# Three sums of a block in one PSUM bank, and one copy of them in the next block

## The chip, the cores and the metric

One Trainium2 chip; the kernel runs on one of its cores. The metric is the time of one execution on the device, in microseconds. Engines are named as in the profile: PE multiplies matrices, PEld is its weight load, DVE is the vector engine, ACT the scalar engine, POOL issues the gathers, SP the other transfers.

## The reference

A graph layer on 6250 nodes with 64 features and 206250 edges, sorted by their destination:

```python
h = jnp.maximum(_layernorm(x, axis=-1), 0.0)
msg = h[src] + edge_attr
agg = jax.ops.segment_sum(msg, dst, num_segments=6250)
out = x + jax.nn.relu(agg @ W1 + b1) @ W2 + b2
```

All of it is fp32. The gather `h[src]` and the sum by destination are what costs.

## The kernel before, in words

The aggregate is kept turned round in SBUF (`agg`, two halves of 64 partitions by node) and is made of two terms. The features gathered from `h` are not gathered at all for most edges: the kernel counts on PE how often each source occurs among a triple of destinations, and multiplies these counts by `h`. The edge features are summed on PE with 0/1 matrices. The last 20 tiles of edges ("groups") go another way: POOL gathers their rows of `h` and adds them to the edge features in flight, and both are summed at once.

Nodes are handled in 23 blocks (`NW`), each of 14 steps (`STEPS`; the last block has 10). The order of all work is written out by hand, step by step, in the loop at the end of the kernel (`for n, (b, s) in enumerate(steps)`), and every engine takes its instructions in this order. In one step stand, in this order:

- `count(b, s)`: six matmuls into one of two PSUM buffers `pc` (L868), and one copy on ACT of 882 columns to the ring of counts (L871). Once in three steps, two comparisons on DVE make the 0/1 matrices for it (L858).
- `multiply(b - 1, ...)`: in steps 0 to 6, the 49 matmuls of the counts of the block before with `h` (L888), into the PSUM tile `pv`.
- `chunk_place` at step 3: twelve matmuls (L461) that put the sums of the edge features of the block before into `pv`, by a selection matrix. After it, at step 10, DVE adds `pv` to `agg`.
- the dense layers of a block that is complete: `mlp_hidden` at step 8 (and 11 if there are two), PE L936 and ACT L938; `mlp_product` two steps later, PE L943 and ACT L949.
- `chunk_sum` at steps 7, 10 and 13 (`SUMS`): the sums of edge features, below.
- `features_h`, at steps 0, 1, 2 or 4 (`GROUPS`) of some blocks, when the gathers have come in: the sum of two groups (PE L489, ACT L492), placed one to four steps later (PE L508, ACT `sum_p` L512).

`chunk_sum(u)` handles a unit of two chunks of 42 nodes: 24 matmuls (48 in the profile) of a 0/1 matrix (`hot`, by DVE, a step earlier) with edge features (`feat`, by SP, two units ahead) into the PSUM tile `bank`, and directly after them ACT copies 128 columns of it to an SBUF tile `by_node` (L442). A block has three units, so three sums and three such copies; the last block has two. `bank` is one tile of 128 columns, used by all units and by the groups in turn:

```python
bank = ps.tile([P, GB * D], F32, name="bank", bufs=1)
...
        by_node[u] = work.tile([P, GB, D], F32, name="by_node", bufs=3)
        nc.scalar.activation(by_node[u][:, :n].rearrange("p c d -> p (c d)"), bank[:, :n * D], AF.Copy)
        load(u + 2)
```

Other work on ACT has places by step number too: clearing `agg` (L162, in blocks 1 and 2), the copies that unpack and turn the keys (`klof` L704, `keys` L726), and checks (`junk` L694). The waits between the engines are put in by a layer that records which instruction touches which tile; for PSUM it keeps two engines apart by the bank.

Of the kernel before, what the change touches and what calls it, by code (L numbers as in the profile page):

```python
# [9 lines left out]
F32 = mybir.dt.float32  # L10
# [4 lines left out]
AF = mybir.ActivationFunctionType  # L15
# [4 lines left out]
P = 128  # L20
N = 6250
E = 206250
D = 64
# [14 lines left out]
GB = 2  # L38
# [8 lines left out]
WQ = 21  # L47
QP = 32
# [28 lines left out]
NW = 23  # L77
# [37 lines left out]
OPEN = 30  # L115
KR = 540
AHEAD = 16
OPENING_US = 15.0


@with_exitstack
def gnn_kernel(ctx: ExitStack, tc: tile.TileContext, x, src_t, dst_t, dst_g, edge, w1, b1, w2, b2, out):
    nc = tc.nc
# [8 lines left out]
    ps = ctx.enter_context(tc.tile_pool(name="ps", bufs=2, space=PSUM))  # L132
    work = ctx.enter_context(tc.tile_pool(name="work", bufs=2))
# [263 lines left out]

    bank = ps.tile([P, GB * D], F32, name="bank", bufs=1)  # L400
    nc.vector.memset(bank, 0.0)
    units = []
    for b in range(NW):
        c0, c1 = (start[b] // CN, min(start[b + 1], NS) // CN)
        units += [(b, c, min(c1 - c, GB)) for c in range(c0, c1, GB)]
    assert sum(n for _, _, n in units) == NC
    unplaced = [sum(1 for unit in units if unit[0] == b) for b in range(NW)]

    def load(u):
        if u >= len(units):  # L410
            return
        _, c, n = units[u]
        at = nc.values_load_multi_w_load_instructions(
            starts_i[0:1, c:c + n], engines=[mybir.EngineType.SP], min_val=0, max_val=G * P * J - CE,
            skip_runtime_bounds_check_because="sums of edges before, at most that by a min")[1]
        feats[u] = [work.tile([P, CT, D], F32, name="feat", bufs=4) for _ in range(n)]
        for k in range(n):
            nc.sync.dma_start(feats[u][k].rearrange("p (q k) d -> p q (k d)", q=JQ),
                              edge[ds(at[k], CE), :].rearrange("(q p k) d -> p q (k d)", p=P, k=JP))

    hot_of = {}
    by_node = {}
# [9 lines left out]
    def chunk_sum(u):  # L432
        n = units[u][2]
        hot, feat = hot_of.pop(u), feats.pop(u)
        for i in range(n):
            for k in range(JP):
                for q in range(JQ):
                    j = q * JP + k
                    nc.tensor.matmul(bank[q * QP:q * QP + WQ, i * D:(i + 1) * D], hot[:, i, j, :], feat[i][:, j, :],  # L439
                                     start=(k == 0), stop=(k == JP - 1))  # L440
        by_node[u] = work.tile([P, GB, D], F32, name="by_node", bufs=3)
        nc.scalar.activation(by_node[u][:, :n].rearrange("p c d -> p (c d)"), bank[:, :n * D], AF.Copy)  # L442
        load(u + 2)

    def column(b, node):
        i, half = node - start[b], NH if b < NW - 1 else HL
        return (i + half) % (2 * half) if 2 * b % 3 == 2 else i

    def runs(b, low, high):
        half = start[b] + (NH if b < NW - 1 else HL)  # L450
        cuts = sorted({low, high} | ({half} if low < half < high and 2 * b % 3 == 2 else set()))
        return [(column(b, a), a, z) for a, z in zip(cuts, cuts[1:])]

    def chunk_place(u):
        b, c, n = units[u]
        of = by_node.pop(u)
        unplaced[b] -= 1
        for i in range(n):
            low = (c + i) * CN
            for k, a, z in runs(b, low, low + CN):  # L460
                nc.tensor.matmul(pvs[b][0][i * D:(i + 1) * D, k:k + z - a], of[:, i, :], select[:, a - low:z - low],  # L461
                                 start=False, stop=False)
# [21 lines left out]
    def sum_groups(g, hot, tiles):  # L484
        for b in range(GB):
            for k in range(PK):
                for q in range(PQ):
                    j = q * PK + k
                    nc.tensor.matmul(bank[q * QP:q * QP + WQ, b * D:(b + 1) * D], hot[:, b, j, :],  # L489
                                     tiles[b][:, j, :], start=(k == 0), stop=(k == PK - 1))  # L490
        by_node["h", g] = work.tile([P, GB, D], F32, name="by_group", bufs=1)
        nc.scalar.activation(by_node["h", g].rearrange("p b d -> p (b d)"), bank, AF.Copy)  # L492

    sels = {}

# [38 lines left out]
    def fetch_pair(i0):  # L534
        n = min(2, IC - i0)
        fetch_words(i0, n, P, [first_i[:, i:i + 1] for i in range(i0, i0 + n)])
# [454 lines left out]
    def pool_until(us):  # L991
        while queue and pool[0] <= us:
            cost, f = queue.pop(0)
            pool[0] += cost
            f()

    def features_h(g):
        read_bases(g, GB)
        sum_groups(g, hot_groups(g), [parts_of.pop(g + b) for b in range(GB)])
        for b in range(GB):  # L1000
            fetch_h(g + 2 * GB + b)
# [70 lines left out]
    for k in range(1, (IC + 1) // 2):  # L1072
        n = (17, 58, 100, 142, 184, 226, 268)[k - 1]
        if k > 2:
            before.setdefault(n - AHEAD, []).append(
                lambda k=k: queue.insert(0, (WORDS_US, lambda: fetch_pair(2 * k))))
# [3 lines left out]
    for t in range(1, NT):  # L1080
        n = (0, 18, 101, 156, 226)[t]
# [8 lines left out]
    def clock(n):  # L1090

        return n * HEAD_US if n < STEPS else STEPS * HEAD_US + (n - STEPS) * STEP_US

    steps = [(b, s) for b in range(NW) for s in range(STEPS if b < NW - 1 else STEPS_L)]
    first_step = [steps.index((b, 0)) for b in range(NW)]
# [4 lines left out]
    SUMS, PLACES, LAYERS = (7, 10, 13), 3, (8, 11)  # L1100
    PRODUCTS = (5, 12, 19, 26, 33, 41, HI)
    PRODUCTS_L = (8, 18, 28, 39, HI)
    ADDED, LOADED = 10, 2
    LAST, LATE, SUMS_L = (3, 8), 7, (6, 8)
    ADDS = (6, 7)
    GROUPS, PLACED = (0, 1, 2, 4), (1, 2, 4, 5)
# [4 lines left out]
    def at(step, f, *a):  # L1111
        later.setdefault(step, []).append(lambda: f(*a))
# [8 lines left out]
    for u, (b, c, _) in enumerate(units):  # L1121
        i = u - min(v for v in range(u + 1) if units[v][0] == b)
        n = (10, 12, 13)[i] if b == 0 else first_step[b] + (SUMS if b < NW - 1 else SUMS_L)[i]
        places.setdefault(b, []).append(u)
        at(n - 1, chunk_hot, u)
        at(n, chunk_sum, u)

    h_next = GA

# [12 lines left out]
    for n, (b, s) in enumerate(steps):  # L1142
# [6 lines left out]
        if b >= 1 and s == (PLACES if b < NW - 1 else 2):  # L1149
            for u in places[b - 1]:  # L1150
                chunk_place(u)
# [4 lines left out]
        k = n - (first_step[SB + 1] + ADDED + 1)  # L1156
# [16 lines left out]
        if n >= 3:  # L1173
# [7 lines left out]
            if n == 3:  # L1181
                pool[0] = clock(n - 1) + OPENING_US
            pool_until(clock(n) + LAND_US)
# [31 lines left out]
    for u in places[NW - 1]:  # L1215
        chunk_place(u)
# [4 lines left out]
    if late_hot is not None:  # L1221
        sum_groups(h_next, late_hot, [parts_of.pop(h_next + b) for b in range(GB)])
# [16 lines left out]
    with tc.If(odd > 0):  # L1239
# [26 lines left out]
        with tc.For_i(0, G, 1) as g:  # L1266
            feat = work.tile([P, J, D], F32, tag="pfeat", bufs=4, name="feat2")
# [17 lines left out]
            with tc.For_i(0, more, 1) as w:  # L1285
                hot = work.tile([P, J, WR], F32, tag="pfeat", bufs=4, name="hotr")
# [7 lines left out]
                at = nc.s_assert_within(first_n + w * WR, 0, N + W - 1)  # L1294
# [44 lines left out]
```

## Time and profile before

| | |
|---|---|
| median of 3 runs | 489.25 us (488.44 to 490.86) |
| the profiled execution | 489.07 us, its span 487.2 us |
| PE busy | 424.2 us (87% of the span) |
| DVE busy | 415.1 us (85%) |
| POOL busy | 388.3 us (80%) |
| ACT busy | 366.0 us (75%) |
| copies of the sums, L442 | 68, together 19.0 us of ACT |

Busy time counts an instruction from its start to its end; on ACT and PE the next one overlaps the end of the one before, so the slots are shorter than the durations. Matmul ends are modelled. A wait is the idle time of an engine before an instruction, put down to what ended it. In the chain that ended last, each piece is what the next one had to wait for, back from the end of the execution. The first some 55 us are loads, the normalization and the sorting of the lists; the steps fill the rest.

### The profile page before, as it was taken

The numbers are of one execution on the slowest core, as the hardware profiler recorded it, in microseconds if no ns is written. First come the engines' busy times: TensorE is split into PE (matmuls) and PEld (weight loads), VectorE is DVE, ScalarE is ACT, GpSimd is POOL, SyncE is SP. The second block draws the span as 40 slices with busy tenths as digits, with TensorE's granted clock in tenths as the row PEclk, the third lists the DMA queues.
The fourth block names the chain that finished last, engine by engine and source line by source line (L and its number), as shares of the span: only waits on it lengthen the run. The fifth ranks groups of instructions, "written<-read, shape, count | busy, mean of one in ns | idle before, by whom it ended". The sixth has DMA issues, their size and how long they took to land.

```text
span 487.2 us, 17218 instructions
## 1 busy us (share of the span) xinstructions
PE 424.2 (87%) x7301; PEld 374.8 (77%) x7302; DVE 415.1 (85%) x561; ACT 366.0 (75%) x607; POOL 388.3 (80%) x239
## 2 busy tenths in 40 slices
PE   3156798998988999999999999989999999999894
PEld 3055687886886888888988978878888888888783
DVE  7888989879999798988998889888998899998751
ACT  3727889878877788788898789777887787786650
POOL 7787888888888888888888888888888888888000
PEclk9655699999999999999999999999999999999998
DMA  9959367378366585784784784675775775764700
GB/s 237 238 172 300 74 147 193 76 180 192 69 167 155 145 228 122 176 230 105 192 220 98 172 228 94 170 201 125 187 187 124 201 179 122 203 158 93 213 13 16
DMA packets 122378, 77.98 MB, mean 160 GB/s; under 512 B 34768, under 2 KB 120728, under 8 KB 122072
## 3 DMA queue, kind: packets, MB, share of 16 engines
q1 hardware_dynamic: 97464, 66.88, 47.1%
q0 software_dynamic: 24592, 9.19, 15.0%
q8 instruction: 59, 0.97, 0.8%
q10 hardware_dynamic: 240, 0.75, 0.5%
q14 instruction: 23, 0.19, 0.1%
HBM read 72.80 MB, written 3.99 MB: 158 GB/s over the span
## 4 chain that ended last, share of the span: by engine, by line
PE 68%; ACT 13%; DMA 6%; issue 5%; DVE 4%; POOL 3%; DVEq 0%; ACTq 0%; POOLq 0%
PE pv L888 26%; PE pc L868 22%; PE bank L439 11%; ACT counts L871 9%; POOL rows L301 3%; DMA feat<-in_edge 3%; PE po L943 2%; PE pv L461 2%; DMA dstq<-in_dst_g,cols_i 2%; ACT junk L694 1%; PE ph L936 1%; PE bank L489 1%; DVE hot_key L858 1%; DVE hot_lo L858 1%; DMA firsts_i<-in_dst_g 1%
## 5 line engine op out<-in xcount | busy, mean ns | idle before, releaser
L301 POOL DMA_INDIRECT pfeat<-table,src_p x160 | 334.0, 2088 | 49.7 <-issue 43.0
L871 ACT ACTIVATE counts<-pc 128x882 fp32r<-128x882 f32 x318 | 282.1, 916 | 49.1 <-PE pc L868 39.8
L868 PE MATMUL pc<-hot_key,hot_lo 128*128 128x147 bf16 x1908 | 179.2, 232 | 22.9 <-ACT counts L871 13.6
L858 DVE TENSOR_TENSOR hot_lo<-iota_lo,keys 128x2304 bf16<-128x2304 bf16 (+1 forms) x107 | 143.8, 1344 | 36.2 <-PE pc L868 29.0
L888 PE MATMUL pv<-counts,h 128*128 128x252 f32 (+1 forms) x1127 | 171.0, 292 | 0.2
L868 PEld LDWEIGHTS <-hot_lo 128*128 128x128 bf16 x1908 | 130.5, 100 | 45.4 <-issue 24.2
L858 DVE TENSOR_TENSOR hot_key<-iota_key,keys 128x2664 bf16<-128x2664 bf16 (+1 forms) x107 | 163.3, 1526 | 0.0
L888 PEld LDWEIGHTS pv<-counts,h 128*128 128x128 f32 x1127 | 143.5, 190 | 0.6 <-ACT counts L871 0.5
L439 PE MATMUL bank<-feat,hot 128*21 128x64 f32 x3240 | 69.0, 222 | 5.9 <-issue 3.0
L439 PEld LDWEIGHTS bank<-feat,hot 128*21 128x21 f32 x3240 | 52.3, 101 | 18.3 <-issue 6.8
L427 DVE TENSOR_TENSOR hot<-rel,iota 128x504 f32<-128x504 bf16 x68 | 45.6, 671 | 0.1
L442 ACT ACTIVATE by_node<-bank 128x128 f32<-128x128 f32 x68 | 19.0, 280 | 18.4 <-PE bank L439 12.4
L301 POOL DMA_INDIRECT words<-packed,first_i x15 | 20.8, 1385 | 4.6 <-issue 3.4
L301 POOL DMA_INDIRECT rows<-in_dst_g,row_i x15 | 17.4, 1162 | 5.2 <-issue 4.0
L943 PE MATMUL po<-w2s,hid 128*126 128x64 f32 (+2 forms) x100 | 16.8, 288 | 1.7 <-ACT hid L938 1.2
L943 PEld LDWEIGHTS po<-w2s,hid 128*126 128x126 f32 (+2 forms) x100 | 13.5, 192 | 5.7 <-ACT hid L938 1.9
L936 PE MATMUL ph<-sums,w1s 128*128 128x252 f32 (+2 forms) x50 | 16.1, 404 | 0.2 <-ACT y L949 0.2
L900 DVE TENSOR_TENSOR sums<-sums,pv 128x252 f32<-128x252 f32 (+4 forms) x31 | 9.8, 339 | 6.7 <-PE pv L888 5.9
L492 ACT ACTIVATE by_group<-bank 128x128 f32<-128x128 f32 x10 | 2.8, 277 | 15.1 <-PE bank L489 11.1
L938 ACT ACTIVATE hid<-ph,b1s 128x252 f32<-128x252 f32 (+2 forms) x25 | 11.6, 464 | 2.3 <-PE ph L936 2.3
L461 PE MATMUL pv<-select,by_node 128*64 128x42 f32 (+1 forms) x272 | 12.6, 234 | 0.0
L461 PEld LDWEIGHTS pv<-select,by_node 128*64 128x64 f32 x272 | 9.9, 137 | 3.0
(202 smaller groups left out, 252.3 us busy)
## 6 DMA issues: line engine op xcount, KB each, us to landing
feat<-in_edge SPq DMA_DIRECT2D x135, 384.0 KB
pfeat<-in_edge SPq DMA_DIRECT2D x20, 256.0 KB
pfeat<-table,src_p POOLq DMA_INDIRECT x160
xl<-in_x SPq DMA_DIRECT2D x2, 768.0 KB
xs<-in_x SPq DMA_DIRECT2D x23, 63.0 KB
out_y<-y SPq DMA_DIRECT2D x23, 63.0 KB
dstn<-in_dst_g SPq DMA_DIRECT2D x1, 1024.0 KB
table<-xl SPq DMA_DIRECT2D x1, 800.0 KB
```

The source lines that it names most:

```text
L301: nc.gpsimd.indirect_dma_start(out=rows, out_offset=None, in_=source, in_offset=bass.IndirectOffsetOnAxis(ap=index, axis=0), compute_op=op)
L427: nc.vector.tensor_tensor(hot_of[u][:, :n].rearrange("p c j w -> p (c j) w"), rel[:, c:c + n].rearrange("p c q k -> p (c q k)").unsqueeze( ...
L439: nc.tensor.matmul(bank[q * QP:q * QP + WQ, i * D:(i + 1) * D], hot[:, i, j, :], feat[i][:, j, :], start=(k == 0), stop=(k == JP - 1))
L442: nc.scalar.activation(by_node[u][:, :n].rearrange("p c d -> p (c d)"), bank[:, :n * D], AF.Copy)
L461: nc.tensor.matmul(pvs[b][0][i * D:(i + 1) * D, k:k + z - a], of[:, i, :], select[:, a - low:z - low], start=False, stop=False)
L858: nc.vector.tensor_tensor(hot[:, :n].rearrange("p t (m o) -> p t m o", o=2), iota_k.rearrange("p (m o) -> p m o", o=2).unsqueeze(1).to_bro ...
L868: nc.tensor.matmul(pc[:, k, m * K:(m + 1) * K], hot_lo[:, j, :], hot_key[:, j, :K], start=True, stop=True)
L871: nc.scalar.activation(ring[:, (2 * b + half) % 3, :, i * ST * V:(i + 1) * ST * V].rearrange("p h (k m) -> p h k m", k=2), pc[:, :, :ST // ...
L888: nc.tensor.matmul(pv[:, :2 * half].rearrange("p (k n) -> p k n", k=2), h2[:, h, :], of[:, :, h, :half], start=(h == 0), stop=(h == HI - 1))
L936: nc.tensor.matmul(ph[:, :n], w1s, agg[:, start[b]:start[b + 1]], start=True, stop=True)
L938: nc.scalar.activation(outs[b][:, :n], ph[:, :n], AF.Relu, bias=b1s)
L943: nc.tensor.matmul(po[:pairs[b], k, :], outs[b][:, k:2 * pairs[b]:2], w2s, start=True, stop=True)
```

## The change

`bank` becomes a full PSUM bank of four sets of 128 columns: three for the units of a block (`set_of[u]` is 0, 1 or 2), one for the groups. `chunk_sum` no longer copies. A new `chunk_copy` copies the sets of a block with one instruction of 384 columns into one tile `by_node[b]`. It stands at step 1 (`COPIED`) of the next block, behind that step's counts and ahead of a group's sum, two steps before `chunk_place` reads it. In the last block each unit is copied at its own step, as before. Loads and matmuls keep their steps.

```diff
-    bank = ps.tile([P, GB * D], F32, name="bank", bufs=1)
+    bank = ps.tile([P, SETS + 1, GB, D], F32, name="bank", bufs=1)
...
+    set_of = [sum(1 for v in units[:u] if v[0] == units[u][0]) for u in range(len(units))]
...
-                    nc.tensor.matmul(bank[q * QP:q * QP + WQ, i * D:(i + 1) * D], hot[:, i, j, :], feat[i][:, j, :],
+                    nc.tensor.matmul(bank[q * QP:q * QP + WQ, set_of[u], i, :], hot[:, i, j, :], feat[i][:, j, :],
                                      start=(k == 0), stop=(k == JP - 1))
-        by_node[u] = work.tile([P, GB, D], F32, name="by_node", bufs=3)
-        nc.scalar.activation(by_node[u][:, :n].rearrange("p c d -> p (c d)"), bank[:, :n * D], AF.Copy)
         load(u + 2)
+
+    def chunk_copy(b, u0, u1):
+
+        if b not in by_node:
+            by_node[b] = work.tile([P, SETS, GB, D], F32, name="by_node", bufs=1)
+        k0, k1 = set_of[u0], set_of[u1] + 1
+        nc.scalar.activation(by_node[b][:, k0:k1].rearrange("p k c d -> p (k c d)"),
+                             bank[:, k0:k1].rearrange("p k c d -> p (k c d)"), AF.Copy)
...
-        of = by_node.pop(u)
+        of = by_node[b][:, set_of[u]]
...
-                    nc.tensor.matmul(bank[q * QP:q * QP + WQ, b * D:(b + 1) * D], hot[:, b, j, :],
+                    nc.tensor.matmul(bank[q * QP:q * QP + WQ, SETS, b, :], hot[:, b, j, :],
...
-        nc.scalar.activation(by_node["h", g].rearrange("p b d -> p (b d)"), bank, AF.Copy)
+        nc.scalar.activation(by_node["h", g].rearrange("p b d -> p (b d)"),
+                             bank[:, SETS].rearrange("p b d -> p (b d)"), AF.Copy)
...
-    ADDED, LOADED = 10, 2
+    ADDED, LOADED, COPIED = 10, 2, 1
...
         at(n, chunk_sum, u)
+        if b == NW - 1:
+            at(n, chunk_copy, b, u, u)
+        elif unplaced[b] == i + 1:
+            at(first_step[b + 1] + COPIED, chunk_copy, b, u - i, u)
```

More of the change, by code (lines that the diff above doesn't have):

```diff
@@ L117 @@
 AHEAD = 16
+SETS = 3
 OPENING_US = 15.0
```

## The prediction

> **What bounds the kernel now.** I read the page's header, then the waits, then the chain that ended last in windows of one block, then the timelines of ACT and PE around every copy that the change touches.
>
> ```profile
> span 487.2 us, 17218 instructions
> PE 424.2 (87%) x7301; PEld 374.8 (77%) x7302; DVE 415.1 (85%) x561; ACT 366.0 (75%) x607; POOL 388.3 (80%) x239
> PE 68%; ACT 13%; DMA 6%; issue 5%; DVE 4%; POOL 3%; DVEq 0%; ACTq 0%; POOLq 0%
> ```
>
> PE is the busiest engine and carries 68% of the chain; ACT carries 13%. So a microsecond taken from ACT is worth something only where PE stands and waits for ACT. The waits (engine, line, what it waited for: us, times, longest) say how much of that there is:
>
> ```profile
> ACT counts L871 <- PE pc L868: 39.8, 92, 1.2
> PE pc L868 <- ACT counts L871: 13.6, 25, 1.4
> ACT by_node L442 <- PE bank L439: 12.4, 23, 1.5
> ```
>
> ACT waits for PE three times as long as PE for ACT. The whole stock from which a lighter ACT can give anything is the 13.6 us of the second row. The copy of the sums itself (third row) mostly stands waiting for PE: it follows the sum in its own step.
>
> Most of those waits have nothing to do with the copies. A block has 14 steps. In steps 0 to 6 PE has the products of the block before and is late; in steps 7 to 13 it has the sums and the dense layers, and is short of work. This is PE in steps 10 to 13 of one block, then ACT over the same time:
>
> ```profile
> 247.06 0.55 PE L868 MATMUL pc<-hot_key,hot_lo 128*128 128x147 bf16 x6 [0.34 <-ACT counts L871]
> 248.85 0.94 PE L868 MATMUL pc<-hot_key,hot_lo 128*128 128x147 bf16 x12
> 250.40 0.55 PE L868 MATMUL pc<-hot_key,hot_lo 128*128 128x147 bf16 x6 [0.61 <-ACT counts L871]
> 249.03 0.28 ACT L442 ACTIVATE by_node<-bank 128x128 f32<-128x128 f32 x1
> 249.44 2.52 ACT L871 ACTIVATE counts<-pc 128x882 fp32r<-128x882 f32 x3
> ```
>
> The second PE row is steps 11 and 12 back to back. Step 13 needs the PSUM buffer of step 11, so it waits for the counts of step 11, which start at 249.44, just when step 11's six matmuls are through (half of 0.94 us after 248.85 is 249.3). The 0.61 us of step 13 is therefore PE's own order and ACT's 0.9 us counts, not the copy at 249.03, and it stays. What the copies can shorten is the wait of step 10 (0.34 here), which is for the counts of step 8, behind the copy of step 7.
>
> **The change, part by part.** The instruction order of the changed build has 24 copies of the sums on ACT in place of 68: one of 384 columns in each of 22 blocks, and two short ones in the last block as before. PE, DVE, SP and POOL keep their instructions in the same order, with the same DMAs.
>
> *ACT's time.* The rows of ACT by shape (count, then busy us, mean ns):
>
> ```profile
> L442 ACT ACTIVATE by_node<-bank 128x128 f32<-128x128 f32 x67 | 18.8, 281 | 18.4 <-PE bank L439 12.4 <-PE pc L868 4.0 <-PE pstart L343 1.0
> L392 ACT ACTIVATE rel<-pdst 128x384 bf16<-128x384 f32 x5 | 2.5, 490 | 2.7 <-issue 1.6 <-PE pdst L391 1.0
> 246.05 0.16 ACT by_node L442
> 246.21 0.81 ACT counts L871
> 247.01 0.04 issue
> 247.06 0.55 PE pc L868 x6
> ```
>
> A short copy lasts 281 ns, but the chain (last four rows, the block above) shows it holding ACT only 0.16 us, since the next instruction overlaps its end. No copy of 384 fp32 columns to fp32 is in the trace; the nearest row reads 384 columns of PSUM and writes bf16: 490 ns. That is 0.21 longer than a short one, so its slot is about 0.37 us. Per block 3 x 0.16 = 0.48 goes and 0.37 comes: 0.11 x 22 = 2.4 us of ACT's 366.0. That alone buys nothing; the place counts.
>
> [...]
>
> *What goes (gain).* On the chain the copies of the sums stand 15 times, from 75.62 to 469.59, with 3.4 us together; first, last but one, and last:
>
> ```profile
> 75.62 0.16 ACT by_node L442
> 393.30 0.28 ACT by_node L442
> 469.59 0.29 ACT by_node L442
> ```
>
> The last is in the last block and stays, which leaves 14 and 3.1 us as the upper bound. What is late next decides how much of it is real. In four of the 14 (near 153, 249, 283 and 286 us) the counts or the layer behind the copy wait for a PE result that comes as late: nothing. In the other ten it is mostly as here, the step-7 copy of one block (PE, then ACT):
>
> ```profile
> 262.54 0.62 PE L868 MATMUL pc<-hot_key,hot_lo 128*128 128x147 bf16 x6
> 263.09 0.28 ACT L442 ACTIVATE by_node<-bank 128x128 f32<-128x128 f32 x1 [0.32 <-PE bank L439]
> 263.26 0.91 ACT L871 ACTIVATE counts<-pc 128x882 fp32r<-128x882 f32 x1
> ```
>
> The counts of step 8 start at 263.26 behind the copy; without it they could start when step 8's matmuls are done, at 262.54 + 0.62 = 263.16 and 0.04 for the signal: 0.06 us gained. At 246.05, where ACT is behind, the full slot of 0.16 is gained. I take 0.13 for each of ten: **-1.3 us** (0.6 to 2.0). The copies at steps 10 and 13 that are not on the chain lie beside PE's work and give nothing.
>
> *What comes (loss).* The long copy stands in ACT's queue behind the counts of step 1. Queued behind it are the counts of step 2, and who waits for those is PE's step 4. ACT in steps 0 to 3 of one block, then PE's step 4:
>
> ```profile
> 214.90 1.95 ACT L871 ACTIVATE counts<-pc 128x882 fp32r<-128x882 f32 x2
> 217.23 0.92 ACT L871 ACTIVATE counts<-pc 128x882 fp32r<-128x882 f32 x1 [0.37 <-PE pc L868]
> 218.51 0.92 ACT L871 ACTIVATE counts<-pc 128x882 fp32r<-128x882 f32 x1 [0.36 <-PE pc L868]
> 219.77 0.56 PE L868 MATMUL pc<-hot_key,hot_lo 128*128 128x147 bf16 x6
> ```
>
> ACT idles 0.37 us just there and 0.36 a step later, and the counts of step 2 end at 218.15, 1.6 us before PE needs them. The slot is covered: 0 in an ordinary block. Without that cover it would be 0.37 a block. The placing matmuls, which read the copy, come in step 3, two steps later, as late as before. Three places are not ordinary:
>
> ```profile
> 64.65 1.70 ACT L871 ACTIVATE counts<-pc 128x882 fp32r<-128x882 f32 x2
> 66.24 1.52 ACT L162 ACTIVATE sums<-zero 128x1591 f32<-128x1591 f32 x1
> 68.11 0.23 PE L717 MATMUL pk<-identb,klof 128*128 128x128 bf16 x1 [0.48 <-ACT klof L704]
> 233.32 1.96 ACT L871 ACTIVATE counts<-pc 128x882 fp32r<-128x882 f32 x2
> 235.13 0.65 PE L489 MATMUL bank<-pfeat,hotp 128*21 128x64 f32 x32
> 421.01 0.39 PE L825 MATMUL pb<-bad,ones 128*128 128x4 f32 x2 [0.31 <-ACT sum_p L512]
> ```
>
> In block 1 (first three rows) the long copy goes between the two counts at 64.65, ACT is behind, and PE already waits 0.48 us at 68.11: **+0.37**. In block 10 a pair of groups is summed at step 1, and the changed build makes that sum wait for ACT, behind the long copy: it is the only group sum there that waits for ACT, where six did before. ACT ends the counts of step 1 at 235.28; the copy, begun some 0.1 earlier, ends near 235.67, and PE would have begun at 235.13: **+0.55**, and PE is the bound behind it. At 421.01 PE waits for a copy that comes right behind the long one: **+0.05** (0.37 if nothing covers).
>
> [...] The sums and the groups now have columns of their own, so by address nothing would conflict. [...] By address the sum below would be 0.55 us lower; by bank it stands, and the build's wait agrees with the bank.
>
> *Sum.* -1.3 + 0.37 + 0.55 + 0.05 = -0.3 us. The profiled execution took 489.07 us (1.9 outside its span of 487.2), 0.2 under the median of 489.25. So 489.07 - 0.3 = **488.8 us**.
>
> **The rivals.** *ACT is worth its full slot (faster).* If the semaphore signals, rather than the modelled ends of PE's matmuls, place the counts right behind each copy, then all 14 pieces go, 3.1 us, and ACT's earlier finish also covers the three losses: 489.07 - 3.1 = 486.0 us, a little less if steps 10 and 13 give as well. For it: ACT carries 13% of the chain and the second wait row has 13.6 us. Against it: most of these waits are the 0.61 us kind that no copy touches. [...]
>
> *The long copy is not covered (slower).* It joins ACT's queue at the busiest point of PE. Where ACT comes to step 1 late by over 1.6 us (groups, key turns and checks on ACT in steps 0 to 4), the 0.37 us passes to PE's step 4, and from there to the end, PE being the bound. In all 22 blocks that is 489.07 - 1.3 + 8.1 = 495.9; in half of them 491.8. For it: block 1 and the 0.31 us at 421. Against it: the two idle times of 0.36 us in an ordinary block.
>
> That the change does less than it says is excluded by the instruction order (24 copies, not 68).
>
> **How the numbers follow.** About 0.5% (2.4 us) is what a measurement of this kernel can tell from no change: the three runs shown lie between 488.44 and 490.86. My forecast, within it: 0.66. The faster rival: 0.20. The slower: 0.14. The range takes in the whole 3.1 us and some scatter downwards, 485.6, and upwards half of the blocks uncovered, 491.8; beyond it I leave about 0.1 at each end.
>
> **What would show it.** Right: ACT's busy time falls by 2 to 4 us and the span by under 1; the 0.61 us waits of PE stay; the 0.2 to 0.35 us waits at step 10 shrink by a little; the long copies last about 0.49 us; a new PE wait of about 0.5 us before the group sum near 235 us, and nearly 0.9 in place of 0.48 near 68 us. Wrong: a span shorter by 2 us or more with PE's total wait for the counts well under 12 us, or PE waits for counts in steps 2 to 6 of ordinary blocks.

## The result, and the profile after

The changed kernel takes 494.6 us in the median of 8 runs (492.0 to 497.6), the kernel before 489.3 us beside it (488.4 to 492.0): ratio 1.0102, 95% interval 1.0066 to 1.0138. It is slower, by 5.3 us, and outside the predicted range. The profiled execution took 497.5 us, its span is 495.6 us; it is one of the two slowest of the eight, so what it shows need not stand in every execution. Some executions further on, of either kernel, fell into a second, slower state; medians and ratios below leave these out.

The head of its page (busy times; the granted clock in 40 slices; the chain's shares):

```profile
span 495.6 us, 17152 instructions
PE 428.4 (86%) x7301; PEld 377.9 (76%) x7302; DVE 415.4 (84%) x561; ACT 359.8 (73%) x563; POOL 394.0 (79%) x239
PEclk9655799999997989999999999999999999999999
PE 70%; ACT 13%; DMA 5%; issue 5%; DVE 4%; POOL 1%; DVEq 0%; ACTq 0%
```

ACT lost 6.2 us of its busy time, and the span grew by 8.4. PE is still the bound, with 70% of the chain. The granted clock dips in slices 13 and 15. In the kernel before it does not:

```profile
PEclk9655699999999999999999999999999999999998
```

The waits between ACT and PE over the counts (ACT's waits for the sums, 12.4 us before, are gone with the short copies):

```profile
ACT counts L880 <- PE pc L877: 63.4, 102, 3.5
PE pc L877 <- ACT counts L880: 16.0, 25, 2.4
```

PE waited 13.6 us for the counts before, the longest 1.4; now 16.0, the longest 2.4. That longest wait stands at step 83 (steps are counted from 0 over all blocks; this is step 13 of block 5). PE, ACT and POOL there:

```profile
151.74 1.20 POOL L302 DMA_INDIRECT words<-packed,first_i  x1 [0.30 <-DVE hot_key L867]
153.02 1.08 PE L877 MATMUL pc<-hot_key,hot_lo 128*128 128x147 bf16 x11 [0.44 <-issue]
154.52 0.23 PE L877 MATMUL pc<-hot_key,hot_lo 128*128 128x147 bf16 x1 [0.42 <-issue]
156.18 1.71 ACT L880 ACTIVATE counts<-pc 128x882 fp32r<-128x882 f32 x2 [3.52 <-PE pc L877]
157.14 0.90 PE L877 MATMUL pc<-hot_key,hot_lo 128*128 128x147 bf16 x6 [2.40 <-ACT counts L880]
```

The six matmuls of step 81 are recorded from 153.02 on and should be through half a microsecond later (six of them take 0.55 us elsewhere in this trace), but ACT, idle since 152.7, is released for their counts only at 156.18. So PE's results came about 2.5 us late, with no wait of PE that the trace names; no copy of the sums is near. I call this the stop; that PE itself stood still is my reading. What follows it, as windows (start:end, length, busy time of each engine, granted clock, DMA share, GB/s):

```profile
155.60:162.40 6.80, 5.26 (x98) 4.42 (x97) 3.50 (x4) 3.54 (x4) 5.88 (x4) 0.50 0.62 156
162.40:176.10 13.70, 12.03 (x169) 10.64 (x166) 8.48 (x10) 8.24 (x12) 11.55 (x8) 1.00 0.56 132
176.10:179.50 3.40, 3.40 (x61) 2.98 (x61) 2.39 (x3) 1.86 (x3) 3.10 (x2) 0.51 0.74 166
```

PE runs at half clock for 6.8 us, and once more for 3.4 us. To see what this costs, I set the start of every step's counting matmuls in one trace against the other and book each change of the difference on its step. Step 83: +2.57 us; steps 84 and 85, at half clock: +0.62 and +1.30. Step 94 (step 10 of block 6): +1.39, before the second stretch begins, so this is a second, shorter stop; step 95, in the stretch: +1.17. PE at step 94:

```profile
176.05 0.90 PE L877 MATMUL pc<-hot_key,hot_lo 128*128 128x147 bf16 x6 [1.52 <-ACT counts L880]
```

So 7.05 of the profiled execution's 8.4 us are two stops and the half clock behind each, a thing that the prediction does not have.

What it does have is there, at its places (timelines of PE and ACT):

```profile
68.73 0.23 PE L726 MATMUL pk<-identb,klof 128*128 128x128 bf16 x1 [0.85 <-ACT klof L713]
242.41 0.48 ACT L450 ACTIVATE by_node<-bank 128x384 f32<-128x384 f32 x1
242.94 0.64 PE L497 MATMUL bank<-pfeat,hotp 128*21 128x64 f32 x32 [0.51 <-ACT by_node L450]
429.17 0.39 PE L834 MATMUL pb<-bad,ones 128*128 128x4 f32 x2 [0.36 <-ACT sum_p L521]
```

0.85 in place of 0.48 at block 1, a new wait of 0.51 ahead of the group sum in block 10, 0.36 in place of 0.31 in block 20.

### The profile page after: what moved, and what is told of

Its sections match the earlier page's. It is cut to its first block, busy times and chain, and to the rows that moved or that the text cites. A ratio compares the mean times of both kernels' runs of the same rounds, so it can differ in the third digit from the quotient of the medians.

```text
span 495.6 us, 17152 instructions
## 1 busy us (share of the span) xinstructions
PE 428.4 (86%) x7301; PEld 377.9 (76%) x7302; DVE 415.4 (84%) x561; ACT 359.8 (73%) x563; POOL 394.0 (79%) x239
## 4 chain that ended last, share of the span: by engine, by line
PE 70%; ACT 13%; DMA 5%; issue 5%; DVE 4%; POOL 1%; DVEq 0%; ACTq 0%
PE pv L897 26%; PE pc L877 23%; PE bank L441 11%; ACT counts L880 9%; PE po L952 3%; DMA feat<-in_edge 2%; PE pv L469 2%; DMA dstq<-in_dst_g,cols_i 2%; PE ph L945 1%; PE bank L497 1%; ACT junk L703 1%; POOL rows L302 1%; ACT inrow L318 1%; DVE hot_lo L867 1%; DMA firsts_i<-in_dst_g 1%
## 5 line engine op out<-in xcount | busy, mean ns | idle before, releaser
L302 POOL DMA_INDIRECT pfeat<-table,src_p x160 | 337.9, 2112 | 50.1 <-issue 43.6
L441 PEld LDWEIGHTS bank<-feat,hot 128*21 128x21 f32 x3240 | 53.3, 103 | 18.3 <-issue 5.9
L302 POOL DMA_INDIRECT rows<-in_dst_g,row_i x15 | 18.8, 1257 | 4.9 <-issue 4.0
L958 ACT ACTIVATE y<-po 126x128 f32<-126x128 f32 (+1 forms) x23 | 6.4, 277 | 9.8 <-PE po L952 7.3
```

The lines of the kernel that those rows point to most:

```text
L302: nc.gpsimd.indirect_dma_start(out=rows, out_offset=None, in_=source, in_offset=bass.IndirectOffsetOnAxis(ap=index, axis=0), compute_op=op)
L441: nc.tensor.matmul(bank[q * QP:q * QP + WQ, set_of[u], i, :], hot[:, i, j, :], feat[i][:, j, :], start=(k == 0), stop=(k == JP - 1))
```

## The experiments

Each batch ran on one chip, with the kernel before beside it. The chips differ: in the first comparison and in batches one, three and five the kernel before takes about 490 us, in batches two and four about 470. I did not find out why; only runs within a batch are compared. Step 4 below is that of block 0.

### Batch one: the place of the copy, its number, the layout

> The changed kernel again, unaltered. Its first profile has two stretches at half the granted TensorE clock inside the steps (6.8 and 3.4 us), which the profile of before has not. Theory 'places' (the waits of step 1 in block 1 and block 10, and later ones like them, cost about 1.3 us, the clock's stretches are chance): runs without such a stretch take 490 to 491 us, and the median falls to about 491. Theory 'pauses' (the change makes PE pause somewhere it did not, and a pause can drop the clock): even the runs without a stretch take 492 us or more, the profile shows a PE wait of over 1 us near 153 us again, and the granted clock is under 0.953 in about half of the runs.

The changed kernel unaltered: 492.3 against 489.7 us, ratio 1.0037 (0.9996 to 1.0077). Its trace has the stop again: +2.52 us at step 83, and the granted clock dips in the same slice 13, to 8 tenths.

```diff
-        if b == NW - 1:
-            at(n, chunk_copy, b, u, u)
-        elif unplaced[b] == i + 1:
-            at(first_step[b + 1] + COPIED, chunk_copy, b, u - i, u)
+        at(n, chunk_copy, b, u, u)
```

> The new PSUM layout alone: sets of columns in one bank, but each sum copied behind its matmuls at its own step, in every block (68 short copies). Theory 'place of the copy' (what costs is the long copy at step 1): as before, ratio 0.997 to 1.003. Theory 'layout' (the wider bank or the different waits on it cost): ratio 1.006 to 1.010, like the full change.

Three copies again, the new layout kept: 491.1 us, ratio 1.0023 (0.9987 to 1.0059), no stop.

```diff
-            at(first_step[b + 1] + COPIED, chunk_copy, b, u - i, u)
+            at(n, chunk_copy, b, u - i, u)
```

> One copy of 384 columns, directly behind the third sum at step 13 of the same block, in place of step 1 of the next. It is off the group sums of step 1 and off the opening's two counts. Theory 'place of the copy': about 1 us under the full change and at most 0.2 us over before (ratio 0.996 to 1.002). Theory 'fewer copies' (ACT without the copies of steps 7 and 10 lets other engines run into a new collision): ratio 1.005 to 1.010, as for the full change.

One long copy, at step 13 of its own block: 491.0 us, 1.0041 (1.0001 to 1.0081), no stop at step 83.

```diff
-    ADDED, LOADED, COPIED = 10, 2, 1
+    ADDED, LOADED, COPIED = 10, 2, 2
...
-            at(first_step[b + 1] + COPIED, chunk_copy, b, u - i, u)
+            at(first_step[b + 1] + (COPIED if b < NW - 2 else 1), chunk_copy, b, u - i, u)
```

> The full change with the long copy at step 2 in place of step 1 (the last block keeps step 1). The group sum of block 10 no longer waits for it. Theory 'place of the copy': 0.5 us under the full change run beside it, no PE wait of 0.5 us near 235 to 243 us; block 1 keeps its 0.4 us. Theory 'fewer copies': no difference from the full change beyond 0.2 us.

One long copy, at step 2 (step 1 in the last block): 490.6 us, 1.0028 (0.9988 to 1.0068), no stop.

These four do not tell the theories apart: the ratios lie within each other's intervals, and the stop is in one trace of four. But each has about the same small loss, 0.2 to 0.4%, though only one interval clears 1, whether it copies once or three times and wherever. So I looked for what all of them share, and compared the traces from their start. The first difference is in the opening. It is a memset, the clearing of the bank (groups by line, kernel before):

```profile
L265 DVE MEMSET spread<- 128x512 f32 x1 | 0.5, 485 | 0.2 <-issue 0.2
L401 DVE MEMSET bank<- 128x128 f32 x1 | 0.2, 165 | 0.0
```

and after:

```profile
L402 DVE MEMSET bank<- 128x512 f32 x1 | 0.5, 485 | 0.1
```

The wider bank takes 0.32 us more to clear, near 9.7 us. DVE and POOL shortly after it, in the kernel before:

```profile
12.54 1.79 POOL L301 DMA_INDIRECT rows<-in_dst_g,row_i  x1 [0.30 <-issue]
13.43 1.22 DVE L598 SCALAR_TENSOR_TENSOR dstn<-dstn,srcl 96x1024 int32<-96x1024 int32 x1
14.64 0.95 POOL L301 DMA_INDIRECT rows<-in_dst_g,row_i  x1 [0.30 <-issue]
14.91 1.22 DVE L598 SCALAR_TENSOR_TENSOR dstn<-dstn,srcl 96x1024 int32<-96x1024 int32 x1 [0.27 <-ACT srcl L595]
```

and after:

```profile
12.33 2.31 POOL L302 DMA_INDIRECT rows<-in_dst_g,row_i  x1 [0.30 <-issue]
13.74 2.35 DVE L607 SCALAR_TENSOR_TENSOR dstn<-dstn,srcl 96x1024 int32<-96x1024 int32 x2
14.94 1.97 POOL L302 DMA_INDIRECT rows<-in_dst_g,row_i  x1 [0.30 <-issue]
```

Before, DVE has a gap of 0.27 us between its two pieces, and POOL's fourth gather, issued in it, takes 0.95 us. After, DVE is 0.3 us later, the gap is closed, and the fourth gather takes 1.97. POOL's fifth gather begins at 17.21 in place of 15.89. In all twenty traces of this study the long memset goes with 2.31 and 1.96 or 1.97 us for gathers three and four (eleven traces), the short one with 1.79 to 1.81 and 0.94 or 0.95 (eight; the ninth has work put on POOL there, and 1.45). Near 46 us, while large loads run (300 GB/s in that slice of the page before), POOL is held in one gather: for 6.1 us in the second gather of features before, for 7.6 in the first after. So it is one gather behind from there on, and a gather of words ("the words gather" below) goes out at 151.74 us in place of 148.74. This is theory "opening"; its rival is "copies".

### Batch two: the memset alone, and the change without it

```diff
-    bank = ps.tile([P, GB * D], F32, name="bank", bufs=1)
-    nc.vector.memset(bank, 0.0)
+    wide = ps.tile([P, 512], F32, name="bank", bufs=1)
+    nc.vector.memset(wide, 0.0)
+    bank = wide[:, :GB * D]
```

> The kernel before with one thing of the change: the clearing of the bank for the sums at the start (a memset on DVE) covers 512 columns in place of 128; nothing else of the change is in it. Theory 'opening': the longer memset (0.49 us in place of 0.17 near 9.7 us) pushes DVE's next pieces into POOL's third and fourth gather of rows (2.3 and 2.0 us in place of 1.8 and 0.95), POOL comes about 1.2 us later to the place near 46 us where it is held for 6 to 8 us, issues one gather fewer before it, and all later gathers of features go out 2 to 3 us later; this meeting of gathers and loads near 152 us is what stops PE at step 83. So: the words gather of 148.7 us comes at 151 to 152, PE stands about 3.4 us at step 83 in place of 0.8, a stretch at half clock follows, span 490 to 495 us, ratio 1.005 to 1.01. Theory 'copies': the stop comes from one long copy at step 1; this kernel has none, so PE stands 0.8 us at step 83, span 487 to 488, ratio 1.000.

The kernel before with the long memset alone: 471.95 against 470.23 us, ratio 1.0036 (1.0015 to 1.0058). Slower, with nothing of the change but the wider tile and its memset; the next run keeps the wider tile. The place of the loss was another than expected: no stop at step 83, but step 4 starts at 48.77 us, in a profiled execution that is the slowest of the twelve (474.5 us).

```diff
-    nc.vector.memset(bank, 0.0)
+    nc.vector.memset(bank[:, 0], 0.0)
...
     nc.vector.tensor_copy(firstp.rearrange("o g q -> o (g q)"), firstp_i)
+    nc.vector.memset(bank[:, 1:], 0.0)
```

> The changed kernel with the memset of the bank in two parts: 128 columns at its old place (0.17 us, as in the kernel before), the other 384 columns later, where DVE stands idle near 16 us. Theory 'opening': the gathers go out as in the kernel before (words gather within 0.5 us of 148.7), PE stands 0.8 us at step 83, no half clock near 155 us; what is left is what the prediction counted and the small waits it did not (+0.4, +0.6, +0.5 us at blocks 1, 10 and 17), span 487.5 to 489, ratio 1.000 to 1.004. Theory 'copies': the stop at step 83 (about 3.4 us) and the half clock behind it stay, span 491 to 496.

The changed kernel with the memset split: 471.06 us, 1.0011 (0.9992 to 1.0029); step 4 at 45.62 us, no stop.

```diff
+    hold = early.tile([P, 1088], F32, name="hold")
     for i in range(6):
         fetch_row(i)
+        if i == 2:
+            nc.gpsimd.memset(hold, 0.0)
```

> The kernel before, with 1.2 us more work on POOL (a memset of a spare tile) between its third and fourth gather of rows near 14 us; nothing of the change is in it. Theory 'opening': the gathers of features go out 2 to 3 us later, PE stands about 3.4 us at step 83, span 490 to 495. Theory 'copies': as the kernel before, 487 to 488. If the memset on DVE gives the stop and this does not, it is not the gathers' phase but something else in DVE's order.

POOL held back by 1.0 us in the opening, in the kernel before: 471.86 us, 1.0030 (1.0006 to 1.0054). It is slower as expected, but its trace has neither the stop nor a late step 4 (45.85 us), so it does not show by which way.

> The changed kernel unaltered, on the chip of this batch, to be compared with the three others. Both theories: gathers 2 to 3 us later than in the kernel before, PE's stand at step 83 about 3.4 us, span 491 to 496, ratio 1.004 to 1.010. A third trace shows how steady the stop is: if it is missing here, chance decides it in each execution.

The changed kernel on this chip: 472.47 us, 1.0029 (1.0010 to 1.0048), the same as the memset alone. No stop; step 4 at 48.77 us. The trace says why step 4 is late (POOL's gather, DVE's wait for it, PE's wait for DVE):

```profile
42.78 0.95 POOL L302 DMA_INDIRECT dstq<-in_dst_g,cols_i  x1 [0.30 <-issue]
46.85 0.42 DVE L384 TENSOR_SCALAR dstq<-dstq,cols 128x384 f32<-128x384 int32 x1 [5.16 <-DMA dstq<-in_dst_g,cols_i]
48.06 0.91 PE L392 MATMUL pdst<-ident,dstq 128*128 128x128 f32 x3 [3.56 <-DVE dstq L385]
```

and with the memset split:

```profile
42.02 1.15 POOL L302 DMA_INDIRECT dstq<-in_dst_g,cols_i  x1 [0.31 <-issue]
42.97 0.42 DVE L384 TENSOR_SCALAR dstq<-dstq,cols 128x384 f32<-128x384 int32 x1 [0.59 <-DMA dstq<-in_dst_g,cols_i]
```

Issued 0.76 us later, the gather is used 3.9 us later. In between, the loads fill the DMA engines, much as they do with the memset split (slice 4 of either page, near 35 to 47 us, has a share of 9 tenths, with 327 GB/s there and 332 here). The window of the changed kernel, columns as above:

```profile
43.00:46.90 3.90, 1.50 (x10) 1.12 (x9) 0.05 (x1) 1.12 (x2) 2.62 (x3) 0.50 1.08 377
```

DVE does 0.05 us of work in 3.9. From block 1 on the two traces stay 3.3 to 3.7 us apart to the end: in this pair the loss is in the opening. But the profiled execution of the changed kernel is the slowest of its twelve (474.8 us), and the medians are only 1.4 us apart, so the other executions need not lose as much there.

### Batch three: the same on a chip of 490 us

> The changed kernel with two edits: the memset of the bank in two parts as in the run with the split (128 columns at its old place, 384 near 16 us), and the long copy at step 2 of the next block (step 1 for the last block). Theory 'opening': the opening is that of the kernel before, the 0.55 us wait of the group sum in block 10 goes, and what is left are the small gains behind the copies of step 7 (0.1 to 0.4 us a place, about 1.3 us in all) against 0.4 us at block 1: ratio 0.997 to 1.000, the best of the four. Theory 'copies': moving the copies by a step does nothing for the opening; ratio as for the changed kernel at step 2, near 1.003.

The split memset, and the copy at step 2 (edits as above): 492.4 against 489.3 us, 1.0059 (1.0024 to 1.0095). A miss; the expected best version is not one. Its trace has no stop and step 4 at 46.18.

```diff
     fetch_dst(0)
-    fetch_pair(2)
     fetch_dst(1)
+    fetch_pair(2)
     fetch_pair(4)
```

> The changed kernel, long memset and all, with one gather moved in POOL's order near 38 to 43 us: the second gather of destinations (dstq) stands ahead of two gathers of words in place of behind them. Theory 'opening', in the form that the last traces gave it: what costs on the path in the opening is this gather, issued at 42.8 us in place of 41.6 and landed at 46.8 in place of 43.9, for which PE's step 4 of block 0 waits (48.8 in place of 45.9 us). With it ahead, step 4 starts at 45.5 to 46 in the profile in spite of the long memset, and the ratio falls to 0.998 to 1.002. Theory 'copies': the ratio stays that of the changed kernel, 1.003 to 1.010.

Step 4 starts at 46.03 us as expected, the ratio does not follow: 494.1 us, 1.0085 (1.0055 to 1.0114). Its trace has the stop (+2.30 us at step 83).

> The changed kernel with the memset in two parts, as run once already, now in one batch with the changed kernel unaltered. Theory 'opening': 0.2 to 0.7% faster than the changed kernel, ratio to the kernel before 1.000 to 1.003; step 4 of block 0 before 46 us and no stop of 3 us at step 83. Theory 'copies': the same time as the changed kernel.

491.3 us, 1.0043 (1.0011 to 1.0074); step 4 at 44.72, no stop.

> The changed kernel unaltered, to be compared with the three others of this batch. Both theories: ratio 1.003 to 1.010. The profile shows which of the two faces of the late gathers this execution had: step 4 of block 0 near 48.8 us, or PE's stop of about 3 us at step 83.

493.7 us, 1.0070 (1.0028 to 1.0111); step 4 at 48.02, no stop. The intervals of split and whole overlap. Set directly against each other, the twelve executions with the whole memset take 2.0 us more in the mean than the twelve with the split one (95% interval 0.2 to 3.8, taken as independent); in batch two it is 1.4 us (0.4 to 2.4). So in the changed kernel too the place of the memset is worth something on both chips. On this chip the change keeps a loss of 0.4% with the memset split.

### Batch four: the memset again, POOL held back, no copies

> The kernel before with the long memset of the bank alone (512 columns in place of 128), once more, on another chip. Theory 'opening': ratio 1.003 to 1.008; the profile has POOL's third and fourth gather at 2.3 and 2.0 us and one of the two faces of the late gathers: step 4 of block 0 at 48 us or later, or the words gather near 151 us with PE's stop of 3.4 us at step 83. Theory 'copies': ratio 0.998 to 1.002 and neither of the two.

472.25 against 469.83 us, 1.0047 (1.0028 to 1.0066): the memset alone makes the kernel before slower on a second chip. The profiled execution (471.2 us, below the median) has step 4 at 45.98 and no stop, so it does not show where.

```diff
+    hold = late.tile([P, 880], F32, name="hold")
+    for _ in range(3):
+        before.setdefault(12, []).append(lambda: nc.gpsimd.memset(hold, 0.0))
```

> The kernel before with its opening untouched and POOL made late by about 2.9 us behind its first two gathers of features (three memsets of a spare tile near 54 us); nothing of the change is in it. In the traces so far the stop at step 83 came in all three in which the words gather went out 2.7 to 3.3 us ahead of that step's place, and in none of the eleven in which it went out 5.8 to 5.9 or 1.0 us ahead, or behind it. Theory 'meeting of gathers and loads': here it goes out about 3 us ahead, so the stop of 2.5 us and the half clock behind it come, span 490 to 495, ratio 1.004 to 1.010. Theory 'copies' (the stop needs the long copies): no stop, ratio 0.998 to 1.002.

471.3 us, 1.0025 (1.0004 to 1.0046), no stop: holding POOL back costs a little here, with nothing of the change. The words gather goes out 6.5 us behind step 83's place, so the question of the stop was not put.

```diff
     def chunk_copy(b, u0, u1):
+        if 0 < b < NW - 1:
+            by_node[b] = by_node[0]
+            return
```

> The changed kernel with the memset in two parts, and without the long copies of blocks 1 to 21: their placements read what block 0 left, so this leaves out part of the computation. It is what the sums' copies can be worth at most. By the prediction's terms: the slots of the copies lie beside other work, so against the run with the split memset it gains only the three waits that were priced (0.4 at block 1, 0.55 at block 10, 0.05 near 421 us) and the one at block 17 (0.5): about 1.5 us, ratio to the kernel before 0.997 to 1.001. By the rival that ACT is worth its full slot: 22 times 0.37, another 5 to 8 us, ratio 0.983 to 0.990.

With the memset split and 21 of the 22 long copies left out (the placements of blocks 1 to 21 read what block 0 left, so part of the computation is missing): 470.4 us, 1.0002 (0.9981 to 1.0023). Even so the kernel is no faster than the kernel before. The sums' copies are not worth a measurable time; the rival of the full slot, 3.1 us or 0.6%, is refuted on this chip.

> The kernel before, unaltered, for a second trace of it: all theories expect the words gather 5 to 6 us ahead of step 83, no stop there, and step 4 of block 0 at 44.5 to 46.2 us (470 or 489 us in all, by the chip). If its gathers stand as in the changed kernel, the opening is a matter of chance in each execution and not of the memset.

One execution, 472.1 us: step 4 at 44.27, no stop. Its words gather is 6.5 us behind step 83, not 5 to 6 ahead: a difference of the chip that the expectation did not have.

### Batch five: the stop without the copies

> The kernel before with its opening untouched and POOL made late by 2.9 us behind its first two gathers of features, once more: in the batch before, the chip was one of those on which the whole kernel takes 470 us, its gathers went out 5 us or more behind step 83's place, not 3 us ahead of it, and the question was not put. On a chip of 489 us they go out about 3 us ahead. Theory 'meeting of gathers and loads': PE stands 3.4 us at step 83 with the half clock behind it, span 490 to 495, ratio 1.004 to 1.010. Theory 'copies': no stop, 0.998 to 1.002. On a chip of 470 us: no stop by either, ratio near 1.0025 as before, and the question stays open.

The trace of the kernel before, with POOL held back by the edit of batch four (POOL, PE, ACT):

```profile
152.26 1.20 POOL L301 DMA_INDIRECT words<-packed,first_i  x1 [0.30 <-DVE hot_key L858]
153.76 0.92 PE L868 MATMUL pc<-hot_key,hot_lo 128*128 128x147 bf16 x10
155.06 0.29 PE L868 MATMUL pc<-hot_key,hot_lo 128*128 128x147 bf16 x2 [0.37 <-issue]
156.75 0.28 ACT L442 ACTIVATE by_node<-bank 128x128 f32<-128x128 f32 x1 [3.38 <-PE pc L868]
157.88 0.29 PE L868 MATMUL pc<-hot_key,hot_lo 128*128 128x147 bf16 x2 [2.53 <-ACT counts L871]
```

The same stop at the same step, +2.55 us, with a lower granted clock behind it (0.91 in the mean of 155.0 to 159.2 us), in a kernel that has nothing of the change. The words gather goes out 3.1 us ahead of the place that step 83 would have without the stop. Over all twenty traces the stop stands in the four with 2.8 to 3.1 us (two of the changed kernel, one with the moved gather, this one), and in none of the sixteen others: 5.8 to 5.9 us ahead (five), 1.0 (three), or behind it (eight). So it needs no long copy. The second stop, at step 94, fits the same pattern: it stands in three traces (the first of the changed kernel, the one with the moved gather, this one), those in which a gather of destinations goes out 2.5 to 2.6 us ahead of that step's place, and in none of the others (0.5 to 0.9 us ahead in three, behind it in fourteen). But the timed runs missed: 492.2 against 491.6 us, ratio 0.9994 (0.9969 to 1.0019). The profiled execution, 496.85 us, is by 2.8 us the slowest of the 13; by their times the others do not seem to have the stop, but there is no trace of them.

> The kernel before with the long memset of the bank alone, once more, in the hope of a chip of 489 us, where the changed kernel had its stop. Theory 'opening': ratio 1.003 to 1.010, and the profile has step 4 of block 0 at 48 us or later, or the stop of 3.4 us at step 83. Theory 'copies': 0.998 to 1.002 and neither.

493.0 us, 1.0010 (0.9980 to 1.0040): undecided. Step 4 at 47.61 us, no stop.

## Why the prediction was wrong

**The step that failed** is the first of the change's parts: "PE, DVE, SP and POOL keep their instructions in the same order, with the same DMAs". The order is the same, but one instruction has another size. The bank is cleared once, and four times the columns are cleared after the change. The trace of before had the price in two rows (165 and 485 ns). These 0.32 us in the opening were left out, and with them what comes behind DVE there: POOL's gathers, which go out later from that place on.

What the missing term is worth: the memset alone cost the kernel before 1.7 and 2.4 us of medians on two chips (0.36% and 0.47%), and an undecided 0.10% on a third; splitting it in the changed kernel gave 1.4 and 2.0 us in the mean. The wider tile itself is not the cause, since the split run has it too. Two ways were seen in the traces, and they leave four of the eleven traces with the long memset without either. A step 4 at 47.6 us or later stands in four of the eleven traces with the long memset and in none of the nine with the short one (44.3 to 46.4). The stop at step 83 stands in three of the eleven, and in one of the nine, the one whose gathers were held back. That the memset acts through the later gathers is so far argued from this and from the two runs with POOL held back, not shown step by step.

**ACT's time** fell by 6.2 us, forecast 2 to 4. The long copy is as forecast (482 ns against 490):

```profile
L450 ACT ACTIVATE by_node<-bank 128x384 f32<-128x384 f32 x22 | 10.6, 482 | 0.0
```

The term that was mis-sized is the slot of the short copy: 0.16 us holds where ACT is behind and the next instruction overlaps its end; elsewhere the full 0.28 counts as busy (the chain itself shows 0.16, 0.28 and 0.29). The time saved bought nothing, as forecast.

**The gain** was forecast at 1.3 us. Between the changed kernel with the split memset and the kernel before, on the chips of 470 us, the booking for blocks 2 to 21 gives -0.3 in all at step 10, and 0.0 at steps 7 to 9. On those of 490 us it is -0.8 at step 10, with +0.5 at step 7 and +0.5 at step 8; the +0.5 of step 7 stands at block 11, where the kernel before with POOL held back has +0.6 too, so these are not all of the copies. PE's whole wait for the counts is 13.7 us there, 13.6 before. So the cleaner pair shows a gain of 0.3 us in place of 1.3: ACT was let go earlier, but PE's waits did not shrink. This is the second term that was mis-sized.

**The losses** were right in place and size: +0.37 us at block 1 (step 4: 68.35 to 68.97 us, of which 0.37 is new), +0.58 at block 10 against 0.55 (the wait for the bank came, 0.51 us, though no column is shared), +0.05 at block 20. The 0.61 us waits of step 13 stayed. In steps 2 to 6 of ordinary blocks nothing was added but 0.50 us at block 17, which the prediction had not. It need not come from the copies: the kernel before with POOL held back has 0.40 there. So the rival of the uncovered copy is out, though its 491.8 to 495.9 us lie close to the measured time: a rival's number can be met for another reason. With the terms as measured, -0.3 + 0.37 + 0.58 + 0.05, the sum would have been +0.7 us, and with the memset's 1.4 to 2.4 us the time would be 491.2 to 492.2 us: about the upper end of the range, and 2.4 to 3.4 us short of 494.6.

**What stays open.** The first comparison's 5.3 us are more than these terms, and more than the changed kernel lost in any of its three repeats (0.37, 0.29 and 0.70%, against 1.02%). The stop can fill the rest in the executions that have it; how often that is, the timed runs do not say. It is hardly all: the fastest of the eight executions, 492.0 us, is 2.7 us above the median before, and its granted clock, 0.956, is not that of the two of 497.5 us (0.946). On a chip of 490 us the changed kernel keeps 0.4% with the memset split, where the measured terms give 0.1 to 0.2%; that rest is not explained. Why POOL's phase differs from execution to execution was not settled either. No version of the change beats the kernel before.

## What to carry to other kernels

When a tile grows, price every instruction that touches it, the one-off ones too, and ask who queues behind them: the cost here was not the 0.32 us itself but 1.4 to 2.4, as far as the traces show by way of the gathers that it delayed. To find such a cost, compare two traces from their start and book the first difference; a view of totals showed only the wait it ended in. And look at more than one execution before explaining a profile: most of what the first trace of the changed kernel showed was two stops that most traces of its relatives do not have.

## What the runs showed of the hardware

POOL's fourth gather of rows took 0.95 us where it began in a gap of DVE's work (14.64 us, before) and 1.97 us where it began beside it (14.94 us, after). POOL's spans are rough, and no run here separates this from other causes.

PE's granted clock fell to 0.50 in the middle of a busy kernel. It did so from 155.6 to 162.4 us, beginning inside the stop in which PE's wait is recorded with 2.40 us, and from 176.1 to 179.5 us, right behind the one with 1.52 us; between the two it was 1.00. It need not fall: behind PE's waits of 1.42 us (for a load, at 61.75) and 1.13 us (for DVE, at 136.75) in the same trace it was 1.00. In the trace of the kernel before with POOL held back, which has the second stop too, the slice that holds it is at 9 tenths, where the 3.4 us at half clock make it 8 in the changed kernel. What made the clock fall, no run shows.

PE's results came late at step 83 or 94, with no wait that the trace names, wherever a gather of words (step 83) or destinations (step 94) had gone out 2.5 to 3.1 us ahead of that step's place: seven times in the twenty traces, and never at these steps otherwise. Other steps were not searched for it. What stops PE there, no run shows.
